# Layer 2's t and p as seven block products instead of eight, in a four-layer float32 network

## The chip, the cores and the metric

The kernel runs on one core of a Trainium2 chip. The core has a matrix engine (TensorE, PE in the profile; PEld is its loading of weights), VectorE (DVE), ScalarE (ACT), GpSimd (POOL) and a DMA-issuing engine (SyncE, SP). They run side by side and wait for one another by semaphores. The metric is the time of one execution on the device, in microseconds (us); lower is better.

## The reference

Four layers run over x of shape (8, 512, 32, 32): 8 batches, 512 channels, 1024 positions. Layer 0 is a normalised bilinear block, layer 1 softmax attention over 512 channels, layer 2 softmax attention over 128 channels, layer 3 a product with signs. All data is float32. The change lies in layer 2, of which this is the part that counts:

```python
xf = x.reshape(n, c, h * w)
proj = jnp.einsum('oc,ncq->noq', W_w, xf) + W_b[None, :, None]
t, p, g = jnp.split(proj, 3, axis=1)
s = jnp.einsum('ncq,nck->nqk', t, p)
s = jax.nn.softmax(s * SCALE, axis=2)
att = jnp.einsum('nqv,ncv->ncq', s, g)
z = jnp.einsum('oc,ncq->noq', Z_w, att)
```

So t and p are each a product of a 128 x 512 weight with x of one batch (512 x 1024), and g is a third one.

## The kernel before

A batch's x lies in on-chip memory (SBUF) as `xt`, four chunks of 128 channels by 1024 positions. `half(0)` and `half(1)` are the two halves of 512 positions. A product into one bank of the accumulator memory (PSUM, eight banks) has 512 columns and sums over chunks of 128 channels.

A first stage (up to about 205 us) makes layer 0's statistics and folds weights. Then `fast` (L813) runs once per batch, eight times, in this order:

- `scores1` (L495): layer 1's scores and exponentials into eight tiles of the pool `epool`, tag `e`, which has eight buffers of 128 x 1024 (`EBUFS`, L80). Tiles `es[0]` to `es[3]` hold the key rows 0 to 511, `es[4]` to `es[7]` the rows 512 to 1023.
- `make_v` (L479): layer 1's values.
- `values1` (L519): layer 1's output, which is added into `xt`. It runs in groups of four products on `L536`: a11·e11, a12·e21, s2·t2, a11·e11 (new contents), a12·e22, a21·e12, a22·e21, each for two row blocks. VectorE takes a group's sum from PSUM (L573, L595, L602, L607), multiplies by the inverse sums (`scaled`, L547), and GpSimd adds the result to `xt` (L549, L575). The quarter of `xt` with chunks 2 and 3 and half 0 is written last, after the last group.
- `project2` (L611): t, p and g of layer 2, which are written into the tile `tpg`. For each half, half 1 first: four products for t, four for p (L621), and sixteen short ones for g (L633). ScalarE and VectorE move them out of PSUM (`evacuate`, L258, and L640). After each of the three, `fill` may run pieces of the next batch's `make_u`: none in half 1, one after each in half 0.
- `scores2` (L748), values (L870) and `close2` (L646) of layer 2, then `leave` (L654), which is layer 3 and stores the output. The second half of `leave` runs inside the next batch's `scores1`.

Beside this, the generator `behind` (L1022) holds the trace chains of layer 0 for later batches (L912, matmuls L925, L926, L959), and `chore` puts pieces of it between the products of `scores1`, `make_v` and `values1`, in the first batches.

Layer 1's products already run in a form with seven block products for eight. `seven` (L314) is a generator that yields after each of its seven terms; a term is made by `product_of` (L358) with two products on L369. `sums_of` (L292) forms sums of the left-hand blocks and `differences_of` (L303) differences of the right-hand blocks. Where the moves out of PSUM combine terms, they run at L320, L322, L326, L328, L331, L341 and L347.

The order of the instructions on each engine is made when the program is built, from the program's order and an estimate of when each can run. A tile of a pool takes a buffer that is released, and waits for it. In the chain stage alone (L1326) PE's order is written out by hand.

`count_bad` (L718) tests the softmax sums once, in the last batch; if the test finds a bad one, `general` (L1392) computes all batches again in a slower way. With the given inputs it doesn't run.

Of the kernel before, what the change touches and what calls it, by code (L numbers as in the profile page):

```python
# [8 lines left out]
F32 = mybir.dt.float32  # L9
# [74 lines left out]
def kernel(  # L84
# [36 lines left out]
    def bank():  # L121
        return psum["bank"].tile([P, HF], F32, tag="bank", name="bank")
# [180 lines left out]
    def differences_of(b, more):  # L303

        b11, b12, b21, b22 = b
        t1, t2, t4 = more
        tt = nc.vector.tensor_tensor
        tt(t1, b12, b11, ALU.subtract)
        tt(t2, b22, t1, ALU.subtract)
        tt(b12, b22, b12, ALU.subtract)  # L310
        tt(t4, b21, t2, ALU.subtract)
        return {"B11": b11, "B21": b21, "B22": b22, "T1": t1, "T2": t2, "T3": b12, "T4": t4}

    def seven(term, c11, c12, c21, c22, b1=None, b2=None, exp=None, then=None):  # L314

# [292 lines left out]
            scaled(u[i], 2 + i, 0)  # L608
            yield

    def project2(env, xt, fill=lambda h: None):  # L611

        big = env["big"]
        tpg = big.tile([P, 3, N], F32, tag="us", name="tpg")
        tt, pt = tpg[:, 0:1, :], tpg[:, 1:2, :]
        gt = tpg[:, 2, :].rearrange("p (t c) -> p t c", c=P)
        for h in reversed(range(NH)):
            for i, dst in enumerate((tt, pt)):
                ps = bank()
                for cc in range(CC):  # L620
                    mm(  # L621
                        out=ps,
                        lhsT=sbw["tpg"][:, cc, bass.ts(i, P)],
                        rhs=xt[:, cc, half(h)],
                        start=cc == 0,
                        stop=cc == CC - 1,
                    )
                evacuate(i, dst[:, 0, half(h)], ps, col("L2_conv_W_b", i))
                fill(h)
            ps = bank().rearrange("p (t c) -> p t c", c=P)  # L630
            for i in range(4):
                for cc in range(CC):
                    mm(  # L633
                        out=ps[:, i, :],
                        lhsT=xt[:, cc, bass.ts(4 * h + i, P)],
                        rhs=sbw["tpg"][:, cc, 2 * P : 3 * P],
                        start=cc == 0,
                        stop=cc == CC - 1,
                    )
            nc.vector.tensor_tensor(  # L640
                gt[:, bass.ts(h, 4), :], ps, bg_row.unsqueeze(1).to_broadcast([P, 4, P]), ALU.add
            )
            fill(h)
        return tt, pt, gt

    def close2(xt, att, h):  # L646

# [70 lines left out]
    def count_bad(env):  # L718

        g = 2 * B * 4
        fine = late.tile([g, NH, P], F32, tag="fine", name="fine")
        other = late.tile([g, NH, P], F32, tag="other", name="other")
        nbad = late.tile([g, 1], F32, tag="nbad", name="nbad")
        nc.vector.tensor_scalar(fine, guard, 1.0 / GUARD, None, ALU.is_gt)
        nc.vector.tensor_scalar(other, guard, GUARD, None, ALU.is_lt)
        nc.vector.tensor_tensor(fine, fine, other, ALU.mult)
        for h in range(NH):
            one = slice(0, g // 2)  # L730
            nc.vector.scalar_tensor_tensor(
                other[one, h, :], guard[one, 1 - h, :], RATIO, guard[one, h, :], ALU.mult, ALU.is_gt
            )
            nc.vector.tensor_tensor(fine[one, h, :], fine[one, h, :], other[one, h, :], ALU.mult)
        nc.vector.tensor_reduce(nbad, fine.rearrange("p h n -> p (h n)"), AX.X, ALU.min)
        nc.vector.tensor_scalar(nbad, nbad, -1.0, 1.0, ALU.mult, ALU.add)
        ps = bank()
        mm(out=ps[0:1, 0:1], lhsT=nbad, rhs=ones2[0:g, 0:1], start=True, stop=True)
        nc.vector.tensor_copy(bad, ps[0:1, 0:1])
        return nc.values_load(bad, min_val=0, max_val=P)  # L740
# [72 lines left out]
    def fast(env, n, hb, ua):  # L813


        b = order[n]
        xt = resident.pop(b)
        more = n + 1 < B
        ahead = iter(())
        count = [0]  # L820

        def chore(every):
            count[0] += 1
            if count[0] % every == 0:
                next(behind, None)

        es = [None] * NT
        for k, _ in enumerate(scores1(env, hb, ua, es)):
            if rest3 and k % 2:
                if next(rest3[0], "end") == "end":  # L830
                    rest3.pop()
                    if more and order[n + 1] not in resident:
                        resident[order[n + 1]] = load_x(order[n + 1])
            if k == 8 and more:
                ahead = entering(n + 1)
            if k >= 11 and k % 3 == 0:
                next(ahead, None)
            chore(2)
        for _ in ahead:
            pass  # L840
        esum = es.pop()
        vt = env["big"].tile([P, NT, C], F32, tag="uv", name="vt")
        r = None
        for _ in make_v(hb, vt):
            if r is None:
                r = inverse_sums(env, esum, n)
            chore(2)
        scratch = env["big"].tile([P, 3, N], F32, tag="us", name="scratch")
        got = []
        steps = iter(())  # L850
        for k, _ in enumerate(values1(env, xt, vt, es, r, scratch)):
            chore(2)
            if k == 5 and more:
                nxt = resident[order[n + 1]]
                hb = split_h(env, normal(env, nxt))
        signs = None
        if more:
            steps = make_u(env, hb, got)
        else:
            signs = unpacked(env)  # L860

        def fill(k=1):
            for _ in range(k):
                next(steps, None)

        tt, pt, gt = project2(env, xt, lambda h: fill(1 - h))
        es, esum = scores2(env, pt, tt, lambda t: fill(t % 2))
        banks, r = [None, None], None

        def values2(h, ts):  # L870
            if banks[h] is None:
                banks[h] = bank()
            for t in ts:
                mm(  # L874
                    out=banks[h],
                    lhsT=gt[:, t, :],
                    rhs=es[t][:, half(h)],
                    start=t == 0,
                    stop=t == NT - 1,
                )  # L880
            if t == NT - 1:
                att = env["small"].tile([P, HF], F32, tag="half_b", name="att")
                nc.vector.tensor_tensor(att, banks[h], r[:, h, :], ALU.mult)
                return att

        dst = channels(out[b])
        fill()
        values2(0, range(0, 1))  # L890
        r = inverse_sums(env, esum, B + n)
        values2(0, range(1, NTH))
        att = values2(0, range(NTH, NT))
        values2(1, range(0, NTH))
        close2(xt, att, 0)
        att = values2(1, range(NTH, NT))
        fill()
        for _ in leave(env, xt, dst, [0], signs):
            fill()
        close2(xt, att, 1)  # L900
        fill(2)
        for _ in steps:
            pass
        rest3.append(leave(env, xt, dst, [1], signs))
        if not more:
            verdict.append(count_bad(env))
            for _ in rest3.pop():
                pass

        return hb, got[0] if more else None  # L910
# [437 lines left out]
    with ExitStack() as main:  # L1348
        psum_pools(main, 0, 8)
        big = main.enter_context(tc.tile_pool(name="big", bufs=1, reuse_waits="tile"))  # L1350
        epool = main.enter_context(tc.tile_pool(name="epool", bufs=EBUFS))
        small = main.enter_context(tc.tile_pool(name="small", bufs=3))
        env.update({"big": big, "e": epool, "small": small})
        got = []
        hb = split_h(env, normal(env, resident[order[0]], True))
        for _ in make_u(env, hb, got):
            pass
        ua = got[0]
        for n in range(B):
            hb, ua = fast(env, n, hb, ua)  # L1360

# [30 lines left out]
    def general(env, xt, b, dst):  # L1392
# [52 lines left out]
                nc.vector.tensor_tensor(xs, ps, xs, ALU.add)  # L1445

        attention(env, rows1, float(C) ** -0.5, apply1)
        tt, pt, gt = project2(env, xt)

        def rows2(ps, t):  # L1450
            for h in range(NH):
# [20 lines left out]
    with tc.If(verdict[0] > 0):  # L1472
        with (
            ExitStack() as stack,
            tc.tile_pool(name="gbig", bufs=1) as big,
            tc.tile_pool(name="gepool", bufs=2) as epool,
            tc.tile_pool(name="gsmall", bufs=2) as small,
        ):
            env = {"big": big, "e": epool, "small": small}
            psum_pools(stack, 2, 4)  # L1480

            for a in weights.values():
                nc.vector.tensor_tensor(a["S3"], a["A11"], a["S3"], ALU.subtract)
            for b in range(B):
                xt = load_x(b)
# [43 lines left out]
```

## Time and profile before

| | |
|---|---|
| time, median of 3 runs | 1999.24 us (1999.21 to 1999.36) |
| the profiled run | 1999.32 us, span 1997.5 us, granted PE clock 0.988 |
| L621, t and p | 256 records, 113.6 us |
| L633, g | 512 records, 59.7 us |
| L536, layer 1's values | 768 records with `e` and `vt`, 334.0 us, and 128 with `scratch`, 56.3 us |
| PE's longest wait in total | 18.3 us in 8 places, L369 for ScalarE's L331 into `vt` |

In a profile line the columns are the line of the program, engine, operation, output and input tiles, shapes and count, then busy time and the mean duration of one, then the idle time of the engine before them and what ended it. A float32 product appears as two records. In a timeline the columns are start and duration in us, engine, line, operation, tiles, shape and count, and in square brackets the idle time before and what ended it. The span is counted from the first to the last instruction on the core, so it is a little less than the time of the run.

### The profile page before, as it was taken

How to read it: one execution, taken by the hardware profiler on the slowest of the kernel's cores; microseconds unless marked ns; L12 is line 12 of the kernel's file. 1: busy time of each engine (PE TensorE's matmuls, PEld its weight loads, DVE VectorE, ACT ScalarE, POOL GpSimd, SP SyncE). 2: the span in 40 equal slices, each digit the busy share in tenths (PEclk: the TensorE clock that was granted, in tenths of full speed). 3: DMA queues.
4: the chain of work that ended last, by engine and by line, in shares of the span. 5: the costliest groups of instructions: out<-in, count | busy, mean ns of one | idle time of the engine just before them, and what ended most of it. 6: DMA issues, size and time to landing. Idle time of an engine off the chain costs nothing.

```text
span 1997.5 us, 16654 instructions
## 1 busy us (share of the span) xinstructions
PE 1936.9 (97%) x6262; PEld 997.3 (50%) x6262; DVE 1111.1 (56%) x1822; ACT 536.6 (27%) x838; POOL 187.9 (9%) x152
## 2 busy tenths in 40 slices
PE   8999899999999999999999999999999999999997
PEld 2377346544465445454465446444545446544653
DVE  3245577437863487536752576337653675256626
ACT  2132222134220342123311432034212431134114
POOL 0000000200011000200011000200020001101110
PEclk9989999999999999999999999999999999999999
DMA  9320000002000020001100020002000110010001
GB/s 330 127 74 1 6 6 11 1 11 85 6 11 0 11 84 17 0 0 32 68 11 1 22 77 13 0 11 85 11 0 1 42 53 11 0 32 21 11 1 54
DMA packets 26711, 66.99 MB, mean 34 GB/s; under 512 B 3760, under 2 KB 4016, under 8 KB 25984
## 3 DMA queue, kind: packets, MB, share of 16 engines
q1 hardware_dynamic: 25968, 65.09, 9.5%
q8 instruction: 51, 0.84, 0.2%
q0 software_dynamic: 224, 0.33, 0.1%
q10 hardware_dynamic: 432, 0.43, 0.1%
q14 instruction: 36, 0.29, 0.0%
HBM read 38.51 MB, written 18.87 MB: 29 GB/s over the span
## 4 chain that ended last, share of the span: by engine, by line
PE 92%; DVE 4%; ACT 3%; issue 1%; DMA 0%; DVEq 0%; ACTq 0%
PE bank L369 37%; PE bank L536 19%; PE bank L874 6%; PE bank L621 6%; PE bank L754 6%; PE bank L1122 4%; PE bank L633 3%; PE bank L650 3%; PE bank L392 2%; PE bank L670 1%; PE bank L925 1%; PE wide L1178 1%; PE bank L1232 1%; PE bank L926 1%; PE bank L775 1%; DVE e L326 1%
## 5 line engine op out<-in xcount | busy, mean ns | idle before, releaser
L536 PE MATMUL bank<-e,vt 128*128 128x512 f32 x768 | 334.0, 593 | 0.0
L536 PEld LDWEIGHTS bank<-e,vt 128*128 128x128 f32 x768 | 145.0, 190 | 175.4 <-issue 171.7
L369 PE MATMUL bank<-ut,h 128*128 128x512 f32 x384 | 183.3, 598 | 4.7 <-ACT e L331 4.7
L369 PE MATMUL bank<-us,hs 128*128 128x512 f32 x256 | 121.3, 596 | 0.5 <-DVE us L298 0.5
L326 DVE TENSOR_TENSOR e<-bank,e 128x512 f32<-128x512 f32 x128 | 87.7, 685 | 61.2 <-PE bank L369 59.9
L874 PE MATMUL bank<-e,tpg 128*128 128x512 f32 x256 | 114.6, 595 | 0.0
L754 PE MATMUL bank<-tpg 128*128 128x512 f32 x256 | 114.6, 592 | 0.0
L369 PEld LDWEIGHTS bank<-ut,h 128*128 128x128 f32 x384 | 70.6, 190 | 87.7 <-issue 73.5
L621 PE MATMUL bank<-xt,tpg 128*128 128x512 f32 x256 | 113.6, 592 | 0.0
L369 PE MATMUL bank<-wo,h 128*128 128x256 f32 x384 | 95.7, 389 | 18.3 <-ACT vt L331 18.3
L761 ACT ACTIVATE e<-bank 128x512 f32<-128x512 f32 x128 | 76.4, 597 | 88.3 <-PE bank L754 88.3
L369 PE MATMUL bank<-h,wu 128*128 128x512 f32 x192 | 92.1, 603 | 3.4 <-DVE h L442 3.4
L326 DVE TENSOR_TENSOR vt<-bank,vt 128x512 f32<-128x512 f32 x64 | 44.0, 687 | 90.2 <-PE bank L369 89.3
L341 POOL TENSOR_TENSOR ut<-ut 128x512 f32<-128x512 f32 x16 | 21.7, 1359 | 734.1 <-ACT ut L322 734.1
L766 DVE TENSOR_TENSOR esum<-esum,e 128x1024 f32<-128x1024 f32 x48 | 58.8, 1226 | 54.8 <-ACT e L761 54.8
L369 PEld LDWEIGHTS bank<-wo,h 128*128 128x128 f32 x384 | 72.4, 193 | 31.1 <-ACT vt L331 21.5
L341 POOL TENSOR_TENSOR e<-e 128x512 f32<-128x512 f32 x32 | 41.6, 1301 | 441.1 <-ACT e L320 388.3
L874 PEld LDWEIGHTS bank<-e,tpg 128*128 128x128 f32 x256 | 48.0, 190 | 63.9 <-issue 63.9
L754 PEld LDWEIGHTS bank<-tpg 128*128 128x128 f32 x256 | 48.6, 190 | 60.8 <-issue 58.6
L621 PEld LDWEIGHTS bank<-xt,tpg 128*128 128x128 f32 x256 | 47.9, 190 | 56.4 <-issue 55.0
L369 PEld LDWEIGHTS bank<-us,hs 128*128 128x128 f32 x256 | 47.3, 190 | 57.5 <-issue 51.4
L660 ACT ACTIVATE sg<-xt,rb 128x512 f16<-128x512 f32 x64 | 43.8, 717 | 103.6 <-DVE xt L652 100.9
(306 smaller groups left out, 2996.4 us busy)
## 6 DMA issues: line engine op xcount, KB each, us to landing
xt<-in_x SPq DMA_DIRECT2D x56, 512.0 KB
out<-both SPq DMA_DIRECT2D x64, 256.0 KB
rfull<-rsum SPq DMA_DIRECT2D x64, 128.0 KB
f_dram<-f SPq DMA_DIRECT2D x8, 256.0 KB
fb<-f_dram SPq DMA_DIRECT2D x8, 256.0 KB
w<-in_w SPq DMA_DIRECT2D x1, 1024.0 KB
q<-in_w_q SPq DMA_DIRECT2D x1, 1024.0 KB
k<-in_w_k SPq DMA_DIRECT2D x1, 1024.0 KB
```

The lines of the kernel that those rows point to most:

```text
L326: nc.vector.tensor_tensor(dst, ps, u, ALU.add)
L341: nc.gpsimd.tensor_tensor(c22, c22, c12, ALU.add)
L369: mm(out=ps[:, q * w : (q + 1) * w], lhsT=lt(ka, kb, q, k), rhs=rhs(ka, kb, q, k), start=first and q == 0 and k == 0, stop=last and k == 1 ...
L536: mm(out=ps, lhsT=a[:, t, bass.ts(r_, P)], rhs=e[t], start=first and t == 0, stop=last and t == NTH - 1, skip_group_check=True,)
L621: mm(out=ps, lhsT=sbw["tpg"][:, cc, bass.ts(i, P)], rhs=xt[:, cc, half(h)], start=cc == 0, stop=cc == CC - 1,)
L633: mm(out=ps[:, i, :], lhsT=xt[:, cc, bass.ts(4 * h + i, P)], rhs=sbw["tpg"][:, cc, 2 * P : 3 * P], start=cc == 0, stop=cc == CC - 1,)
L650: mm(out=ps, lhsT=sbw["z"][:, bass.ts(oc, P)], rhs=att, start=True, stop=True)
L754: mm(out=ps, lhsT=pt[:, 0, bass.ts(t, P)], rhs=tt[:, 0, half(h)], start=True, stop=True,)
L761: nc.scalar.activation(e[:, half(h)], ps, AF.Exp, scale=float(P) ** -0.5)
L766: nc.vector.tensor_tensor(esum, esum, e, ALU.add)
L874: mm(out=banks[h], lhsT=gt[:, t, :], rhs=es[t][:, half(h)], start=t == 0, stop=t == NT - 1,)
L1122: mm(out=banks[i][side(h), :], lhsT=w0[i][:, cc, :], rhs=xt[:, cc, half(h)], start=cc == 0, stop=cc == CC - 1,)
```

## The change

- `project2` becomes a generator. It forms four differences of the quarters of `xt` with `differences_of`, in four tiles `xd` from the pool of the exponentials (tag `e`). `xt` itself stays unchanged, since the third difference gets a tile of its own.
- t and p (rows) over the two halves (columns) are then made by `seven`, with 256 x 512 weights in quarter blocks and the two biases: seven terms of two products each take the place of sixteen products.
- After them come the two blocks of g, half 1 first. `fill` runs one piece after the seventh term and one after each block of g.
- The weights' sums are formed once, ahead of the batches: three in a new tile `sp` of 3 x 2 x 128 columns, one in place in the weights for p.
- The two scratch tiles of `count_bad` move to the tags `half_a` and `half_b` of the pool `small`.
- In the conditional part, `epool` has four buffers instead of two, and only the weights of layer 1 are restored.

```diff
     def differences_of(b, more):
 
         b11, b12, b21, b22 = b
-        t1, t2, t4 = more
+        t1, t2, t4, t3 = (list(more) + [b12])[:4]
         tt = nc.vector.tensor_tensor
         tt(t1, b12, b11, ALU.subtract)
         tt(t2, b22, t1, ALU.subtract)
-        tt(b12, b22, b12, ALU.subtract)
+        tt(t3, b22, b12, ALU.subtract)
         tt(t4, b21, t2, ALU.subtract)
...
-    def project2(env, xt, fill=lambda h: None):
+    def project2(env, xt, made):
...
+        wa = weights["tp"]
+        xb = differences_of(
+            [xt[:, chunks[k], half(n)] for k in range(2) for n in range(2)],
+            [env["e"].tile([P, 2, HF], F32, tag="e", name="xd") for i in range(4)],
+        )
+        term = product_of(lambda a, b, q, k: wa[a][:, k, :], lambda a, b, q, k: xb[b][:, k, :])
+        yield from seven(
+            term,
+            tt[:, 0, half(0)],
+            tt[:, 0, half(1)],
+            pt[:, 0, half(0)],
+            pt[:, 0, half(1)],
+            col("L2_conv_W_b", 0),
+            col("L2_conv_W_b", 1),
+        )
         for h in reversed(range(NH)):
-            for i, dst in enumerate((tt, pt)):
-                ps = bank()
-                for cc in range(CC):
-                    mm(
-                        out=ps,
-                        lhsT=sbw["tpg"][:, cc, bass.ts(i, P)],
-                        rhs=xt[:, cc, half(h)],
-                        start=cc == 0,
-                        stop=cc == CC - 1,
-                    )
-                evacuate(i, dst[:, 0, half(h)], ps, col("L2_conv_W_b", i))
-                fill(h)
...
-            fill(h)
-        return tt, pt, gt
+            yield
+        made.extend((tt, pt, gt))
...
-        fine = late.tile([g, NH, P], F32, tag="fine", name="fine")
-        other = late.tile([g, NH, P], F32, tag="other", name="other")
+        fine = env["small"].tile([g, NH, P], F32, tag="half_a", name="fine")
+        other = env["small"].tile([g, NH, P], F32, tag="half_b", name="other")
...
-        tt, pt, gt = project2(env, xt, lambda h: fill(1 - h))
+        made = []
+        for k, _ in enumerate(project2(env, xt, made)):
+            fill(k > 5)
+        tt, pt, gt = made
...
+        sp = late.tile([P, 3, 2, P], F32, tag="sp", name="sp")
+        tp = quarters_of(sbw["tpg"], chunks, [slice(0, P), slice(P, 2 * P)])
+        weights["tp"] = sums_of(tp, [sp[:, i] for i in range(3)])
         for n in range(B):
             hb, ua = fast(env, n, hb, ua)
```

More of the change, by code (lines that the diff above doesn't have):

```diff
@@ L309, in differences_of @@
         tt(t2, b22, t1, ALU.subtract)
-        tt(b12, b22, b12, ALU.subtract)
+        tt(t3, b22, b12, ALU.subtract)
         tt(t4, b21, t2, ALU.subtract)
-        return {"B11": b11, "B21": b21, "B22": b22, "T1": t1, "T2": t2, "T3": b12, "T4": t4}
+        return {"B11": b11, "B21": b21, "B22": b22, "T1": t1, "T2": t2, "T3": t3, "T4": t4}
     def seven(term, c11, c12, c21, c22, b1=None, b2=None, exp=None, then=None):
@@ L1447, in general @@
         attention(env, rows1, float(C) ** -0.5, apply1)
-        tt, pt, gt = project2(env, xt)
+        made = []
+        for _ in project2(env, xt, made):
+            pass
+        tt, pt, gt = made
         def rows2(ps, t):
@@ L1475 @@
             tc.tile_pool(name="gbig", bufs=1) as big,
-            tc.tile_pool(name="gepool", bufs=2) as epool,
+            tc.tile_pool(name="gepool", bufs=4) as epool,
             tc.tile_pool(name="gsmall", bufs=2) as small,
@@ L1480 @@
             psum_pools(stack, 2, 4)
-            for a in weights.values():
+            for a in (weights["u"], weights["o"]):
                 nc.vector.tensor_tensor(a["S3"], a["A11"], a["S3"], ALU.subtract)
```

## The prediction

> **What bounds the kernel now.** I read the page first: its busy line, its chain of waits, its costliest groups.
>
> ```profile
> span 1997.5 us, 16654 instructions
> ...
> PE 1936.9 (97%) x6262; PEld 997.3 (50%) x6262; DVE 1111.1 (56%) x1822; ACT 536.6 (27%) x838; POOL 187.9 (9%) x152
> ...
> PE 92%; DVE 4%; ACT 3%; issue 1%; DMA 0%; DVEq 0%; ACTq 0%
> ...
> L621 PE MATMUL bank<-xt,tpg 128*128 128x512 f32 x256 | 113.6, 592 | 0.0
> ```
>
> The matrix engine (PE) is busy for 97% of the span and is 92% of the chain that ended last. Line 621, which makes t and p, has no idle time before it: what is taken out of it leaves the chain unless a new wait replaces it. The 256 records belong to 2 outputs x 2 halves x 4 chunks x 8 batches = 128 products, so each float32 product is two records.
>
> Then I read the PE timeline where a batch goes from layer 1's values (L536) to t, p and g. I take the batch at 1500 us, which has no trace-chain work in between. Columns are start, duration, engine, line, operation, tiles, shape, count.
>
> ```profile
> 1488.74 11.32 PE L536 MATMUL bank<-e,vt 128*128 128x512 f32 x26
> 1499.90 7.03 PE L621 MATMUL bank<-xt,tpg 128*128 128x512 f32 x16
> 1506.77 3.73 PE L633 MATMUL bank<-tpg,xt 128*128 128x128 f32 x32
> 1510.34 3.60 PE L621 MATMUL bank<-xt,tpg 128*128 128x512 f32 x8
> 1513.77 1.88 PE L369 MATMUL bank<-h,wu 128*128 128x512 f32 x4
> ```
>
> 16 records take 1506.77 - 1499.90 = 6.87 us, so a record costs 0.4294 us and a 512-column product 0.859 us. (The 592 ns of the group row is the life of one overlapped record, not its spacing.) PE has no gap here, and follows the program's order.
>
> Last I read VectorE (DVE) and GpSimd (POOL) over the same stretch, since the added subtractions have to fit there.
>
> ```profile
> 1493.23 0.69 DVE L602 TENSOR_TENSOR o_b<-bank,o_b 128x512 f32<-128x512 f32 x1 [2.01 <-PE bank L536]
> 1493.96 0.69 DVE L547 TENSOR_TENSOR o_b<-o_b,rfull 128x512 f32<-128x512 f32 x1
> 1496.67 0.69 DVE L607 TENSOR_TENSOR o_a<-bank,o_a 128x512 f32<-128x512 f32 x1 [2.02 <-PE bank L536]
> ...
> 1500.10 0.69 DVE L607 TENSOR_TENSOR o_a<-bank,o_a 128x512 f32<-128x512 f32 x1 [2.01 <-PE bank L536]
> ```
>
> ```profile
> 1494.73 1.27 POOL L549 TENSOR_TENSOR xt<-xt,o_b 128x512 f32<-128x512 f32 x1 [2.17 <-DVE o_b L547]
> 1498.17 1.27 POOL L549 TENSOR_TENSOR xt<-xt,o_a 128x512 f32<-128x512 f32 x1 [2.17 <-DVE o_a L547]
> 1501.60 1.26 POOL L549 TENSOR_TENSOR xt<-xt,o_a 128x512 f32<-128x512 f32 x1 [2.17 <-DVE o_a L547]
> ```
>
> DVE works 1.4 us and then waits 2.0 us for PE, over and over. The lower half 1 of x (block B22) is complete at 1494.73 + 1.27 = 1496.00, the lower half 0 (B21) at 1502.86. The upper blocks B11 and B12 are finished earlier.
>
> **What the Trainium skill says.** "SBUF — State Buffer", section "Who interferes with whom": a VectorE two-input operation with both inputs in SBUF and a GpSimd operation that reads SBUF exclude each other, and the second waits for the whole of the first. The trace agrees: POOL's L575 add takes 2445 ns on average where DVE is dense, L549 takes 1266; the difference, 1.18 us, is about one 1.22 us subtraction. I use this for the upper bound below. "VectorE: DVE Perf Modes", section "Why tensor_tensor can't do 2×_2P or 4×": a tensor-tensor in float32 runs at single rate. The trace has 1218 ns for 1024 elements (L308) and 685 for 512, so no cheaper price is to be had for the differences. "Perfetto Trace Analysis", section "Identifying the Most-Contended Engine", warns that PE busy time doesn't measure nearness to the peak; so I price PE by the spacing of starts, not by its share.
>
> **The change part by part.**
>
> Removed: 16 products per batch on L621 (32 records). Added: seven terms of two products, 14 of the same shape (28 records). PE: -2 x 0.859 = -1.72 us a batch, x 8 = **-13.74 us**. The g products and the three fills inside the function stay.
>
> New waits on PE. From 1499.90 each term takes 1.72 us, in the order A11·B11, S2·T2, S3·T3, S1·T1, A12·B21, S4·B22, A22·T4. Needed: T2 at 1501.62, T3 at 1503.34, T1 at 1505.05, B21 at 1506.77, T4 at 1510.21. Available:
> - T1..T4 go into four buffers of the exponentials. All eight are taken by layer 1's exponentials. The four lower ones (key rows 0 to 511) are last read by the a21·e12 groups, which end just before 1493.23; the four upper ones are read to the end of L536.
> - With the lower four, and T1 only after L602 and L547 at 1494.65: T1 to 1495.87, T2 from 1496.00 to 1497.22, T3 to 1498.44. T4 needs B21: 1502.86 to 1504.08. Margins: 4.4 us for T2, 4.9 for T3, 3.9 for B21, 6.1 for T4.
> - Upper bound: each subtraction excludes a POOL add (+1.2 us each way), and L607 and L547 (1.4 us) run ahead of T2 and T3. Then T2 is ready near 1499.8, T3 near 1501.1 to 1502.4, B21 near 1504.1, T4 near 1506.6. All are still before their times. I take 0; the lower end is 0 too, since no PE wait stands here now to be removed.
>
> Behind these waits on DVE stand L607 and L547 of the last two groups and then the moves out of PSUM. Those who wait are POOL's add for B21 (margin above) and PE through banks: seven terms hold four of eight banks, so none is short.
>
> DVE load per batch: four subtractions 4 x 1.22 = 4.88; four combining moves at 0.69, 0.69, 0.745, 0.745 (rows L326, L328) = 2.87; less two evacuations of 0.75 (L262). Net +6.25 us, 50 over the kernel. DVE is busy 6.98 us of the 22.4 from 1489.6 to 1512, so it lies beside PE: 0. ScalarE: one copy 0.59 and two moves at 0.68, less two of 0.69: +0.58 a batch. POOL: one add 1.27. Both engines stand mostly idle here (0.69 and 5.07 us of the 22.4): 0.
>
> End of the block: scores need all of t and p. After the seventh term come three fills (1.72 each) and two g blocks (3.43 each), 12 us; the last combining move takes 0.75: 0.
>
> Weights, once: four DVE operations on 256 columns. No such row; nearest are 128 columns at 315 ns (L953) and 512 at 685, so I interpolate 0.44 each, 1.8 us in all. DVE idles 4.53 us just before 234.97 in the first product of the loop, and the operands came by DMA long before. From 0 (inside that gap) to 1.8 (ahead of the first scores' moves); I take 0.
>
> The two scratch tiles of the final test move into the small pool's rings of three: eight short operations in DVE order. A ring slot could hold back one relu of the last batch: -0.3 to +1 (one L693 is 0.72); I take 0. The code in the conditional fallback isn't executed. No DMA is added or moved.
>
> Sum: 1997.5 - 13.74 = 1983.8 for the span. The same run took 1999.32 and the median is 1999.24, about 1.7 more: **1985.5 us**.
>
> **The rivals.**
>
> A, slower: the four buffers come free only with the last value group, because the subtractions get the upper tiles or are queued behind L607 at 1500.10. Then L607 and L547 to 1501.5, T1 to 1502.7, T2 to 1503.9; S2·T2 starts 2.3 us late, T3 (1505.1) just makes it. Net +2.3 - 1.72 = +0.6 a batch, +4.7: 2003.9. It decides once T2 is later than 1503.34, 6.1 us after my time. For it: all eight buffers are in use and DVE runs in order. Against: the lower four are released first, and their reads end 6.9 us before those of the upper.
>
> B, half given back: in the first three batches the trace chains (L925 to L959) need DVE too, and PE already waits 3.9 us for their evictions; the scheduled orders of DVE and ScalarE shift, and waits of about 0.9 us appear per batch, in this stretch or at the start of v, where PE waits 18.3 us for ScalarE's L331 now. Half of 13.74 lost: 1992.4. Against: DVE's idle pieces of 2 us recur every 3.4 us, and between the chain's last step of the values and the next lie some 90 us.
>
> C, no change: 1.7 us of gap per batch, 1999; the same as B, worse. Another engine becoming the bound isn't credible: DVE goes to 1161 of 1984.
>
> **How the numbers follow.** Forecast 0.76, B 0.12, C 0.04, A 0.08. The likeliest case spans 1983 to 1988: 1.8 and 1 for the unknown costs and the scatter of the schedule. The 8-in-10 range goes from 1982.5 (a few of the present 18.3 us of waits vanish by shifted order) to 1991, into B. A measurement here can tell about 0.2%, 4 us, from no change. Faster 0.87 (forecast, nearly all of B), same 0.05 (C and the edges of B and A), slower 0.08.
>
> **What would show it.** In the profile after: L621 gone; 224 records on L369 reading tpg, the new weight sums, x and the differences; total PE records down by 32 in 6262; DVE near 1161, POOL near 198. If I am right PE's waits name no difference (L309 to L312 writing e) as releaser, or under 0.3 us each. A shows as about 2 us before the second term in every batch; B as longer waits on L331 or L947. I am wrong if T2 is written after 1503 in this batch's time, or if the subtractions run beside a slower PE.

## The result and the profile after

| | before | changed |
|---|---|---|
| time, median | 1999.30 us (1999.21 to 1999.52, 4 runs) | 1989.74 us (1989.2 to 1992.58, 4 runs) |
| ratio, 95% interval | | 0.9955 (0.9938 to 0.9972) |
| span of the profiled run | 1997.5 us | 1987.4 us |

The changed kernel is faster by 9.6 us, and the interval of the ratio lies wholly below 1. The forecast of 1985.5 us was 4.2 us too low, inside its range. The page's busy line:

```profile
PE 1924.2 (97%) x6230; PEld 989.9 (50%) x6230; DVE 1161.0 (58%) x1874; ACT 541.5 (27%) x846; POOL 205.0 (10%) x160
```

PE has 32 records fewer and is still busy for 97% of the span; the page's chain by engine is the same as before, with PE at 92%. VectorE is up by 49.9 us. This is PE's timeline over the new block, in the same batch as was read before:

```profile
1490.52 1.88 PE L369 MATMUL bank<-xt,tpg 128*128 128x512 f32 x4
1492.23 1.88 PE L369 MATMUL bank<-xd,sp 128*128 128x512 f32 x4
1493.95 1.88 PE L369 MATMUL bank<-xd,tpg 128*128 128x512 f32 x4
1495.67 1.88 PE L369 MATMUL bank<-xd,sp 128*128 128x512 f32 x4
1497.38 1.88 PE L369 MATMUL bank<-xt,tpg 128*128 128x512 f32 x4
1499.10 1.88 PE L369 MATMUL bank<-xt,sp 128*128 128x512 f32 x4
1500.82 1.88 PE L369 MATMUL bank<-xd,tpg 128*128 128x512 f32 x4
1502.53 1.88 PE L369 MATMUL bank<-h,wu 128*128 128x512 f32 x4
```

Seven terms in 1502.53 - 1490.52 = 12.01 us, no bracket with idle time among them: PE waits for none of the differences, and its whole list of waits names none in any batch. VectorE's timeline has those differences (tile `xd`) in between the work on the value groups:

```profile
1481.75 1.22 DVE L308 TENSOR_TENSOR xd<-xt 128x1024 f32<-128x1024 f32 x1
...
1486.64 1.23 DVE L309 TENSOR_TENSOR xd<-xt,xd 128x1024 f32<-128x1024 f32 x1 [1.37 <-POOL xt L549]
1487.79 1.22 DVE L310 TENSOR_TENSOR xd<-xt 128x1024 f32<-128x1024 f32 x1
...
1493.60 1.23 DVE L311 TENSOR_TENSOR xd<-xt,xd 128x1024 f32<-128x1024 f32 x1 [1.38 <-POOL xt L549]
```

T2 (L309) is ready at 1486.64 + 1.23 = 1487.87 and wanted at 1492.23.

What was given back stands in PE's list of waits. Of its longest entries, two differ from before (columns: engine and tile of the one that waited, whom it waited for, us in total, times, longest):

```profile
PE bank L369 <- ACT vt L331: 18.3, 8, 3.7
...
PE bank L742 <- DVE nbad L740: 4.6, 1, 4.6
PE bank L369 <- DVE h L442: 4.6, 1, 4.6
```

L742 is the one product of the final test, `nbad` the result that it needs (L738 and L736 in the kernel before, where no wait stands there). L442 is the normalisation ahead of the first batch, for which PE waited 3.4 us before. These are PE's and VectorE's timelines at the end of the last batch:

```profile
1963.69 3.60 PE L654 MATMUL bank<-att,z 128*128 128x512 f32 x8
1971.91 0.19 PE L742 MATMUL bank<-ones,nbad 64*1 64x1 f32 x2 [4.62 <-DVE nbad L740]
1972.03 6.26 PE L674 MATMUL bank<-sg,signs 128*128 128x512 f16 x16
```

```profile
1961.05 0.27 DVE L731 TENSOR_SCALAR other<-guard 64x256 f32<-64x256 f32 x1
...
1968.32 0.75 DVE L705 SCALAR_TENSOR_TENSOR both<-up,ps,both 128x512 f32<-128x512 f32 x1
...
1969.59 0.28 DVE L730 TENSOR_SCALAR fine<-guard 64x256 f32<-64x256 f32 x1
```

In the program L730 (`fine`) comes ahead of L731. Here it runs 8.5 us after it, behind the use (L705) of the last of the four results in `up`, which share the ring `half_a`. A ring is a tag's set of buffers, here three, which its tiles take in turn. In the kernel before the test's last VectorE operation (L736) was over at 1973.72, ahead of layer 3's first L689 at 1975.84, and PE's product had no wait before it:

```profile
1981.75 0.19 PE L738 MATMUL bank<-ones,nbad 64*1 64x1 f32 x2
```

To see where the time goes I cut every profiled run at four marks of PE's timeline: the start of the s2·t2 group (L536 with `scratch`) in batches 1, 4 and 8, and the start of the last `close2` (L650, now L654). All figures are us, and differences of starts; the last column runs to the end of the span and is given to a tenth.

| kernel | batch 1 to 4 | batch 4 to 8 | batch 8 to last `close2` | to the end |
|---|---|---|---|---|
| before | 685.55 | 852.51 | 90.77 | 19.3 |
| changed | 679.79 | 845.64 | 89.05 | 23.7 |
| changed, second profile | 679.92 | 845.64 | 89.05 | 23.3 |

Four batches save 6.87 us and the last one 1.72, so each saves 1.72. The end loses 4.4.

### The profile page after: what moved, and what is told of

Its sections match the earlier page's. It is cut to its first block, busy times and chain, and to the rows that moved or that the text cites. A ratio compares the mean times of both kernels' runs of the same rounds, so it can differ in the third digit from the quotient of the medians.

```text
span 1987.4 us, 16731 instructions
## 1 busy us (share of the span) xinstructions
PE 1924.2 (97%) x6230; PEld 989.9 (50%) x6230; DVE 1161.0 (58%) x1874; ACT 541.5 (27%) x846; POOL 205.0 (10%) x160
## 4 chain that ended last, share of the span: by engine, by line
PE 92%; DVE 4%; ACT 3%; issue 1%; DMA 0%; DVEq 0%; ACTq 0%
PE bank L369 41%; PE bank L536 19%; PE bank L881 6%; PE bank L758 6%; PE bank L1129 4%; PE bank L637 3%; PE bank L654 3%; PE bank L392 2%; PE bank L674 2%; PE bank L932 1%; PE bank L1239 1%; PE wide L1185 1%; PE bank L933 1%; PE bank L779 1%; DVE e L326 1%
## 5 line engine op out<-in xcount | busy, mean ns | idle before, releaser
L536 PE MATMUL bank<-e,vt 128*128 128x512 f32 x768 | 334.0, 593 | 0.0
L536 PEld LDWEIGHTS bank<-e,vt 128*128 128x128 f32 x768 | 145.0, 190 | 175.4 <-issue 173.2
L369 PE MATMUL bank<-wo,h 128*128 128x256 f32 x384 | 96.2, 390 | 18.3 <-ACT vt L331 18.3
L787 DVE RECIPROCAL rsum<-bank 128x512 f32<-128x512 f32 x16 | 53.7, 3358 | 24.1 <-PE bank L779 24.1
L1129 PE MATMUL bank<-xt,fg 128*64 128x512 f32 x256 | 59.1, 611 | 5.3 <-DMA fg<-in_w_fg 5.3
```

The source lines that it names most:

```text
L369: mm(out=ps[:, q * w : (q + 1) * w], lhsT=lt(ka, kb, q, k), rhs=rhs(ka, kb, q, k), start=first and q == 0 and k == 0, stop=last and k == 1 ...
L536: mm(out=ps, lhsT=a[:, t, bass.ts(r_, P)], rhs=e[t], start=first and t == 0, stop=last and t == NTH - 1, skip_group_check=True,)
L787: nc.vector.reciprocal(r, ps)
L1129: mm(out=banks[i][side(h), :], lhsT=w0[i][:, cc, :], rhs=xt[:, cc, half(h)], start=cc == 0, stop=cc == CC - 1,)
```

## The experiments

The theory is that PE sets the time in this block, that the differences are hidden with some 4 us to spare because four buffers come free early, and that what is missing from 13.7 us was given back at the final test (4.4 us) and at the weights' sums (1.2 us). The rivals are that the differences cost PE something in each batch, that the buffers don't matter, or that the two waits have other causes.

**1. The test's scratch out of the rings.** The changed kernel, with `fine` and `other` in the tile of the weights' sums:

```diff
-        fine = env["small"].tile([g, NH, P], F32, tag="half_a", name="fine")
-        other = env["small"].tile([g, NH, P], F32, tag="half_b", name="other")
+        fine = env["sp"][0:g, 0]
+        other = env["sp"][0:g, 1]
...
-        sp = late.tile([P, 3, 2, P], F32, tag="sp", name="sp")
+        sp = env["sp"] = late.tile([P, 3, 2, P], F32, tag="sp", name="sp")
```

> The changed kernel, with the two scratch tiles of the final test taken out of the small pool's rings and laid into the weight sums' tile, which is idle by then. Theory (the ring slot of fine comes free only when the last relu of the last batch is consumed, so the test's eight short operations run late and its product makes PE wait): the 4.6 us wait of PE before L742 is gone, the stretch from the last L654 to the end goes back from 23.7 to 19.3 us, and the time falls by 4.4 us to about 1985.3. Rival (the wait is for the guard's DMA or for VectorE's other work, whatever the slots): the wait stays and the time stays at 1989.7.

Measured: 1986.76 us (1984.91 to 1988.83), ratio to before 0.9941 (0.9927 to 0.9954), span 1982.9. PE's timeline at the end of the last batch:

```profile
1963.60 3.60 PE L654 MATMUL bank<-att,z 128*128 128x512 f32 x8
1967.13 0.19 PE L742 MATMUL bank<-ones,nbad 64*1 64x1 f32 x2
```

The wait is gone, and the stretch to the end is 1982.9 - 1963.60 = 19.3 us, as expected. The median fell by 3.0 us instead of 4.4; the intervals of the two kernels overlap, so that the wait is gone is shown by the trace, and its worth in the time is not shown by the medians alone.

**2. This part alone, in the kernel before.**

```diff
-        fine = late.tile([g, NH, P], F32, tag="fine", name="fine")
-        other = late.tile([g, NH, P], F32, tag="other", name="other")
+        fine = env["small"].tile([g, NH, P], F32, tag="half_a", name="fine")
+        other = env["small"].tile([g, NH, P], F32, tag="half_b", name="other")
```

> The kernel before, with this part of the change alone: the two scratch tiles move into the rings half_a and half_b. Theory: 4.4 us slower than before, about 2003.7, with a PE wait of 4 to 5 us before L738. Rival (the wait comes with the seven terms, not with the rings): 1999.3, no wait.

Measured: 2002.59 us beside 1998.81 for the kernel before, ratio 1.0018 (1.0011 to 1.0024). That is 3.8 us slower where 4.4 was expected; from the last L650 (start 1978.52) to the end of the span of 2001.4 it takes 22.9 us, 3.6 more than before. PE's list of waits has the same entry, which the seven terms can't have made:

```profile
PE bank L738 <- DVE nbad L736: 4.6, 1, 4.6
PE bank L369 <- DVE h L442: 3.4, 1, 3.4
```

**3. The weights' sums on GpSimd.**

```diff
-    def sums_of(a, more):
+    def sums_of(a, more, eng=None):
...
-        tt = nc.vector.tensor_tensor
+        tt = (eng or nc.vector).tensor_tensor
...
-        weights["tp"] = sums_of(tp, [sp[:, i] for i in range(3)])
+        weights["tp"] = sums_of(tp, [sp[:, i] for i in range(3)], nc.gpsimd)
```

> The changed kernel, with the four operations that form the weights' sums on GpSimd instead of VectorE. Theory (on VectorE they slipped in ahead of the first batch's normalisation, L220 to L442, and hold up the first product): PE's wait for L442 goes from 4.6 back to 3.4 us and the time falls by 1.2 us to about 1988.5. Rival (that wait differs for another reason, the granted clock or the chain before it): 4.6 us stays, 1989.7.

In the changed kernel VectorE's timeline shows the four at 206.25 to 207.81, ahead of the steps that lead to the normalisation. In the kernel before, L220 followed L423 directly, with 0.20 us of idle time between them:

```profile
206.25 0.42 DVE L297 TENSOR_TENSOR sp<-tpg 128x256 f32<-128x256 f32 x1
...
207.72 0.17 DVE L220 RECIPROCAL r_r<-r_e 128x4 f32<-128x4 f32 x1
```

Measured: PE's wait for L442 is 3.2 us instead of 4.6, as expected. The time is 1990.57 us (1988.91 to 1992.01), which shows no gain. The trace shows why little was to be had. GpSimd's four run from 201.47 to 204.81, and two short VectorE steps on the way to PE's products end only when one of these ends. One is:

```profile
203.63 1.18 POOL L300 TENSOR_TENSOR sp<-tpg,sp 128x256 f32<-128x256 f32 x1
204.15 0.68 DVE L414 TENSOR_TENSOR dev<-mv,mean 128x4 f32<-128x4 f32 x1
```

L414 takes 0.16 us in the changed kernel, and L411 0.49 here for 0.16 there. PE's waits for these steps grow, before L412 from 0.6 to 0.9 us and before L419 from 2.5 to 3.1. From VectorE's L405 to the first product behind L442 it takes 8.05 us here, 8.30 in the changed kernel and 7.12 in the kernel before. So the cause of the longer wait for L442 is shown, but this run gives back 0.25 of the 1.2 us: on GpSimd the sums stand in the way at another place.

**4. Both together**, in two runs, the second beside the changed kernel itself.

> Both: scratch in the weight sums' tile and the sums on GpSimd. Theory: the two add up to 5.6 us, about 1984.1, which is the 13.7 us of the matrix engine with nothing given back. Rival (the end is set by something else once the wait is gone): above 1986.

> The changed kernel itself beside the others on one chip: 1989.7 within 1.5 us.

> Scratch in the weight sums' tile and the sums on GpSimd, beside the changed kernel on the same chip. Theory: both waits gone, 4 to 5.6 us under the changed kernel, and under the kernel before by 13 us. Rival (the scatter of the first stage is all there is between them): the same within 1.5 us.

Measured: 1986.30 and 1986.46 us; the changed kernel beside the second, 1989.11 (1988.66 to 1992.68). Against the kernel before, the pair has 0.9939 (0.9926 to 0.9953) and 0.9934 (0.9920 to 0.9947), the changed kernel 0.9954 (0.9940 to 0.9968). The wait at the test is gone in both traces (19.6 and 19.3 us to the end), and the wait for L442 is 3.2 and 3.4 us. In the second run the median is 2.7 us under the changed kernel's, not 5.6. Its trace and that of the changed kernel beside it differ at the end alone: the s2·t2 group of batch 1 starts at 350.57 and 350.59 us, batches 1 to 4 take 680.02 and 679.92, and the end 19.3 and 23.3. So the expected sum was too high by the sums' 1.2 us, which GpSimd doesn't give back (run 3); what lies between 4.0 us in the traces and 2.7 in the medians is within the scatter. Runs 1 and 4 are the fastest versions measured, and can't be told apart.

**5. Without the differences.**

```diff
-        xb = differences_of(
-            [xt[:, chunks[k], half(n)] for k in range(2) for n in range(2)],
-            [env["e"].tile([P, 2, HF], F32, tag="e", name="xd") for i in range(4)],
-        )
+        b11, b12, b21, b22 = (xt[:, chunks[k], half(n)] for k in range(2) for n in range(2))
+        xb = {"B11": b11, "B21": b21, "B22": b22, "T1": b12, "T2": b22, "T3": b12, "T4": b21}
```

> The changed kernel without the four subtractions of x: the terms take x's own blocks in their place, so t and p are not what they should be (this part is left out); the products, the moves out of PSUM and the weights' sums stay. Theory (the subtractions lie wholly beside PE): the same time as the changed kernel, 1989.7 within 1.5 us, with VectorE's busy time down by 39. Rival (they cost PE something in each batch): 4 us or more faster.

This kernel leaves the differences out, so its t and p are not those of the reference. Measured: 1990.81 us (1989.13 to 1992.52), VectorE 1124.4 us. Batches 4 to 8 take 845.66 us, against 845.64 with the differences: they cost nothing there.

**6 and 7. The differences twice, and four times.**

```diff
-        tt = nc.vector.tensor_tensor
+        tt = lambda *k: [nc.vector.tensor_tensor(*k) for _ in range(2 if len(more) > 3 else 1)]
```

(with 4 in place of 2 for the second; only the new differences have more than three tiles)

> The changed kernel with each of the four subtractions done twice, one right after the other in the program. Theory (T2 and T3 have a margin of some 4 us): VectorE's busy time is up by 39 us, no PE wait names a subtraction for more than 0.3 us, and the time is the changed kernel's, 1989.7 within 2 us. Rival (margin under 2.4 us): 1 us or more per batch, above 1997.

> The changed kernel with each subtraction done four times. By the margin of 4 us, sixteen operations of 1.22 us can't all be done in time: the third difference is due 1.7 us after the second and comes some 5 to 9 us late. Theory: PE waits 5 to 9 us per batch for a subtraction, 2030 to 2062. Rival (the differences are never on PE's path, whatever their length): 1989.7.

Measured: twice, 1992.32 us (1991.85 to 1992.87), a little over the 2 us allowed. VectorE is at 1204.6 us. PE waits for a difference once, 0.8 us; batches 4 to 8 take 845.65 us, so the excess isn't there but in the first three batches (681.48 us for 1 to 4) and in scatter. The margin holds a doubling.

Four times: 2088.58 us, ratio 1.0448, which is 12.4 us a batch over the changed kernel, more than the 5 to 9 expected. PE's timeline in one batch:

```profile
1553.71 1.88 PE L369 MATMUL bank<-xt,tpg 128*128 128x512 f32 x4
1557.15 1.12 PE L369 MATMUL bank<-xt,tpg 128*128 128x512 f32 x2 [1.56 <-POOL xt L549]
1561.08 2.07 PE L369 MATMUL bank<-xt,tpg 128*128 128x512 f32 x2 [2.81 <-POOL xt L549]
1562.95 2.55 PE L369 MATMUL bank<-xd,sp 128*128 128x512 f32 x4
1568.98 3.78 PE L369 MATMUL bank<-xd,tpg 128*128 128x512 f32 x4 [3.48 <-DVE xd L307]
1572.55 2.86 PE L369 MATMUL bank<-xd,sp 128*128 128x512 f32 x4
```

The waits in brackets are 7.9 us. But the four records at 1568.98 also take 3.57 us to the next start instead of 1.72: here the products themselves are slower after a wait. The expectation had only the waits. PE's order is another here too (the fifth term, A12·B21, went ahead of the second), and the first two waits are for GpSimd's last adds into `xt`, which wait in turn for VectorE, where the longer differences run.

**8. Rival A built on purpose: late buffers.**

```diff
-        wa = weights["tp"]
+        wa, xd = weights["tp"], big.tile([P, 4, 2, HF], F32, tag="uv", name="xd")
...
-            [env["e"].tile([P, 2, HF], F32, tag="e", name="xd") for i in range(4)],
+            [xd[:, i] for i in range(4)],
```

(and two buffers again in the fallback's pool, which doesn't run)

> The changed kernel with the four differences in the buffer of layer 1's values (tag uv), which comes free only when the last value group has been read: rival A of the prediction, built on purpose. Theory (early release of the four lower exponentials' buffers is what hides the subtractions): PE waits 1.5 to 2.7 us per batch after the first term, 12 to 22 us in all, 2002 to 2011, which is slower than before. Rival (the buffers don't matter, the scheduled order fills the gap): 1989.7.

Measured: 2011.53 us (2011.31 to 2011.91), ratio 1.0063 (1.0046 to 1.0080): slower than before, by the change's own mechanism with one pool exchanged. VectorE's timeline in the batch at 1503 us has the last value group (L607) and then the first difference:

```profile
1503.15 0.69 DVE L607 TENSOR_TENSOR o_a<-bank,o_a 128x512 f32<-128x512 f32 x1 [2.02 <-PE bank L536]
1503.75 1.22 DVE L308 TENSOR_TENSOR xd<-xt 128x1024 f32<-128x1024 f32 x1
```

The loss over the changed kernel is 21.8 us, 2.7 a batch, the upper end of what was expected. The order of PE's instructions changed as well (the fifth term went ahead of the second), so this run shows the effect of late buffers together with the order that was made for them. PE's list of waits names a difference once, for 0.2 us; the longest in this block is for GpSimd's last adds into `xt`, which the fifth term needs (L549, 7.4 us in six places).

**9. An eighth term.**

```diff
             col("L2_conv_W_b", 1),
         )
+        term(None, "A22", "T4", True, True)
         for h in reversed(range(NH)):
```

> The changed kernel with an eighth term in each batch (two more products of the same shape into a bank that nobody reads), so that all of the change is there but for the saving on PE. Theory (a term costs its 1.72 us and nothing in this stretch hides it): PE has 32 records more, 13.7 us slower than the changed kernel, about 2003.5; and slower than before by what the test and the sums give back. Rival (PE isn't the limit in this stretch): less than 7 us slower.

Measured: 2004.89 us (2002.06 to 2006.92) beside 1989.11 for the changed kernel and 1998.86 for the kernel before; ratio to before 1.0030 (1.0019 to 1.0042). Batches 4 to 8 take 852.50 us, those of the kernel before 852.51. A term costs its full price, and the rest of the change costs nothing in these batches. Against the kernel before it is 6.0 us slower, about the 5.6 that the test and the sums were said to give back. The medians of this and the changed kernel lie 15.8 us apart, 2 more than the price of the terms; this lies in the early part, which varies (batches 1 to 4 take 685.71 us here and 685.55 before).

## Why the prediction was right, and where it was off

- **PE, -13.74 us: right.** Each batch after the first three takes 6.87 / 4 = 1.72 us less; with run 9's eighth term the 1.72 us are back in full.
- **Margins: right.** Predicted 4.4 us for T2, 4.9 for T3, 3.9 for B21, 6.1 for T4. In the batch above: 1492.23 - 1487.87 = 4.4; 1493.95 - 1489.01 = 4.9; 1497.38 - 1493.57 (end of POOL's last add) = 3.8; 1500.82 - 1494.83 = 6.0. T1 ran earlier than I placed it, between two value groups, and held back one POOL add there (2.18 us instead of 1.27). That is the exclusion for which I had quoted the Trainium skill, "SBUF — State Buffer", section "Who interferes with whom". It is also why POOL rose by 17 us where I had 10. Nobody waited for that add.
- **VectorE +50, ScalarE +4.6: right** (49.9 and 4.9).
- **Weights' sums: off.** Of the bounds 0 and 1.8 us I took 0, because there was an idle gap of 4.5 us further on. The order that was made put them earlier, just ahead of the steps PE was waiting for: 1.2 us, from the two traces; run 3 shows the cause, though not a gain in the time. The price of one operation, 0.44, was good (0.42).
- **The test's scratch: the step that failed.** I priced a held-back ring slot as one relu, -0.3 to +1 us, and took 0. It cost 4.4 us at the end in the changed kernel (run 1) and 3.6 in run 2. The ring decides not only when one short operation runs but behind what: `fine` came behind the whole first half of layer 3, all of the test's operations but `other` (they are nine, not eight) followed it, and the test's product stands in PE's order ahead of the second half of layer 3, so sixteen products waited with it.
- **The sum.** With the two terms at what they measured, -13.7 + 4.4 + 1.2 = -8.1 us; the spans differ by -10.1. The other -2.0 lies in the first stage and the first three batches, which vary from run to run (batches 1 to 4 of the kernels with seven terms, runs 7 and 8 apart: 679.4 to 683.1 us). That the forecast missed by 4.2 us and not by 5.6 is therefore luck: what it left out was in part hidden by scatter.
- **Rivals.** A's mechanism is real and was rightly kept: with late buffers it made the kernel slower (run 8), and 2.7 us a batch is near the 2.3 worked out, though by another order of the terms. It didn't happen in the changed kernel: its first difference was written at 1481.75, well before the last read of the upper four buffers. B expected half to be given back in the batches with trace chains; no wait of that kind appeared, L331 stayed at 18.3 us. C, no change, didn't happen either. What was given back had other places.

## What to carry to other kernels

A product saved on the engine that sets the end is worth its spacing in the trace, times the count, if everything new is ready by the time it is wanted: write both times for every operand, as a table of margins. Buffers borrowed from a stage that is just ending are free only as early as that stage's last read of them, and this, with the order that came of it, here separated a gain of 10 us from a loss of 12 (run 8). And look at the small tiles that were moved to make room: a tile put into a ring shared with a later stage takes its place behind that stage, and one test at the end of the kernel took back a third of the gain.

## What the runs showed of the hardware

A wait of PE can cost more than its length, since PE's granted clock can fall after it. These are stretches of run 7 around its waits (columns: stretch, its length, busy us and records of PE, PEld, DVE, ACT and POOL, then the granted PE clock as a share of full speed, DMA share, GB/s):

```profile
1557.40:1560.80 3.40, 0.87 (x2) 0.04 (x1) 3.40 (x4) 0.00 (x0) 1.94 (x1) 1.00 0.00 0
1560.90:1564.30 3.40, 3.22 (x4) 1.51 (x5) 3.40 (x3) 0.69 (x1) 0.13 (x1) 0.50 0.00 0
1567.70:1574.50 6.80, 5.52 (x7) 2.43 (x8) 3.65 (x5) 0.00 (x0) 0.00 (x0) 0.50 0.00 0
```

PE was busy for 3.22 + 5.52 = 8.7 us at half the clock, and a float32 record took up to 3.57 / 4 = 0.89 us instead of 0.43. As an estimate from these figures, half of the 8.7 us is lost, 4.4 us; with the 7.9 us of waits this makes 12.3, beside the 12.4 us that a batch lost.

At the end of the kernel the same wait of 4.62 us stands in the changed kernel and in run 2. This is the changed kernel just after it, and run 2's sixteen products:

```profile
1972.00:1977.00 5.00, 5.00 (x14) 1.79 (x13) 1.65 (x3) 2.08 (x3) 0.00 (x0) 0.50 0.01 3
```

```profile
1986.86 5.31 PE L670 MATMUL bank<-sg,signs 128*128 128x512 f16 x16
```

In the changed kernel the clock was at half for 6.8 us and the sixteen products took 6.26 us; in run 2 it was at half for 3.4 us and they took 5.31. The end lost 4.4 and 3.6 us, so here the wait cost less than its length, and how much depended on the clock.

The Trainium skill, "TensorE: Matmul & The Clock Gate", section "What's actually happening", states that the clock is halved after an idle window of about 3.4 us and comes back after a busy one, with windows that run free of the kernel. The traces agree with the length: from 250 us on, every stretch at half clock in the changed kernel, run 2 and run 7 is 3.4 or 6.8 us long, but for the one that the end of the span cuts off. But a window needn't be wholly idle: in run 7 the clock fell after 3.40 us in which PE was busy for 0.87 (first line above), and no wait there was longer than 2.81 us. In the later batches of the kernel before, a lone wait of 1.64 us at the start of `make_v` left the clock at 1.00.

The free-running window would also account for the scatter between runs. In the first three batches the wait at the start of `make_v` is 3.7 us, and the clock falls at it for 3.4 us in some profiles and 6.8 in others. From 520 to 560 us the granted clock is 0.96 in the kernel before and 0.91 in runs 2 and 9, which have as many products there; from s2·t2 of batch 1 to that of batch 2 they take 236.4, 238.7 and 238.7 us. From 760 to 800 us it is the other way round, 0.91 and twice 0.96, and batch 2 to 3 takes 233.0, 230.9 and 230.9 us. The eight profiles of kernels with seven terms, runs 7 and 8 apart, are sorted by the clock in the same way: 234.8 to 234.9 us at 0.96 and 235.6 to 237.1 at 0.91, then 229.3 to 230.0 at 0.96 and 230.5 to 231.7 at 0.91. So the clock goes with the scatter of these batches in all eleven profiles; no run set the clock to show that it is the cause.
